# Third SAGE pass with the turn and copy of an older unit ahead of the step, and a head that adds half of its sums by an identity product

## The chip, the cores and the metric

The kernel runs on one core of one Trainium2 chip. The metric is the device time of one execution in microseconds; each kernel is run several times, and the median stands for it. One execution is also taken by the hardware profiler, and all the times inside a kernel come from that one trace: they are microseconds from the start of its span, or nanoseconds where that is said. TensorE is called PE, VectorE DVE, ScalarE ACT, GpSimd POOL and SyncE SP in the profile.

## What is computed

For 16 graphs of 1024 nodes with 128 features, two layers are applied, each as `x = layernorm(x + layer(x))`. The first is a gated graph network (a GRU over four steps). The second is three SAGE passes with batch norm between them, and a linear head on the three results side by side. Cut to the part that the change touches:

```python
def _sage(x, adj, Wr, Wx, b, mf):
    deg = jnp.clip(jnp.sum(adj, axis=-1, keepdims=True), 1.0, None)
    agg = jnp.einsum('bij,bjd->bid', adj, x) / deg
    out = agg @ Wr + x @ Wx + b
    nrm = jnp.maximum(jnp.linalg.norm(out, axis=-1, keepdims=True), NORM_EPS)
    return out / nrm * mf[..., None]

h3 = _bn(jax.nn.relu(_sage(h2, adj_d, Wr3, Wx3, b3, mf)), g3, be3)
xc = jnp.concatenate([h1, h2, h3], axis=-1) * mf[..., None]
return (xc @ Wl + bl) * mf[..., None]
...
x = _layernorm(x + _L1_gnn_ref(x, adj, nodemask, ...), axis=-1)
```

Batch norm takes its mean and variance over all the nodes of all the graphs, so the head can't begin before the third pass has ended.

## The kernel before

The order of the work on every engine is written out by hand: each engine executes its instructions in the order in which the code records them, and waits where one needs the result of another engine or a buffer that is still in use. The last three stages of the kernel are the third pass, a short set-up and the head.

**The third pass** (`third`, L1806) works on 32 units: 16 graphs times two halves `f` of 512 nodes. The products with the adjacency were made in the pass before and lie in DRAM; `load_layer` (L1693) fetches them for a graph, a graph ahead, on SP's queue. Step `i` of the loop does this, in this order:

- `out_next` (L1728) for unit i on TensorE: four products for the neighbours (`q_oa`, L1734), four of the degree row (`q_ob`, L1737) and four of the node itself against two weights at once (`q_ob`, L1740). A product of float32 stands in the trace as two records.
- `rows` (L1384 to L1391) for unit i-2 on VectorE: three small operations on the norms and one of 128x512 that makes the normalised rows `s_r`.
- `chain` (L1743) for unit i: ScalarE divides `q_oa` by the degree (`scale_rows`, L1370, four times), VectorE adds `q_ob` (L1373), ScalarE squares and sums (`squares`, L1380, four times, each with a record that reads the accumulator) and takes a root (L1381). Then VectorE adds the other half of `q_ob` to the running sums of the head (`s_acc`, L1833).
- for unit i-3: TensorE turns `s_r` (`turned`, L1402, four transposes), ScalarE copies the result out of PSUM into `r3` (L1837) and VectorE takes its batch-norm statistics (L1838).

The PSUM pool of the pass has two buffers each of `q_oa` (one bank), `q_ob` (two banks) and `s_tr` (one bank)[...].

**The set-up** (`batch_norm`, L1305 to L1310, and `head_weights`, L1347) aggregates the statistics, scales the head's third weight (`s_wr`, L1313) and makes `r48`, 48 rows for the constant part (L1320 to L1327), with small products between (`s_v`, L1355 and L1358).

**The head** (`last`, L1841) goes over the 16 graphs. For graph b, `head(b)` makes in each half four products of a mask with a row picked for the graph (`u_rb` by VectorE, L1853; products L1864) and four of `r3` with the weight (L1867), all into one bank `u_p`. VectorE adds `s_acc` to it (L1869), which gives `u_y`, and takes the layer norm's statistics, four of them (L1872) and four aggregates (L1874). ScalarE takes a root for the graph (L1876). `norm(b)`, recorded after `head(b + 1)`, makes scale and shift on VectorE (L1881, L1882), applies them on ScalarE in eight instructions of 128x128 (L1885) and sends 512 KB to the output on SP's queue (L1887). After it comes a flag (`flagged`, L1916).

Of the kernel before, what the change touches and what calls it, by code (L numbers as in the profile page):

```python
# [8 lines left out]
F32 = mybir.dt.float32  # L9
# [5 lines left out]
AF = mybir.ActivationFunctionType  # L15
ALU = mybir.AluOpType
AX = mybir.AxisListType
ET = mybir.EngineType
PSUM = bass.MemoryType.PSUM
DRAM = bass.MemoryType.DRAM  # L20

P = 128
B = 16
# [18 lines left out]
def rows_of(ap):  # L42

    return ap.rearrange("(k p) c -> p k c", p=P)
# [1149 lines left out]
class Sage:  # L1194
# [479 lines left out]
    def second(self):  # L1674

        nc, tc = self.nc, self.tc
        with ExitStack() as c:
            pool = lambda name, **k: c.enter_context(tc.tile_pool(name=name, **k))
            self.wk = pool("q_wk", bufs=2)
            self.big = pool("q_at", bufs=2)  # L1680
            self.ps1 = pool("q_ps1", bufs=1, space=PSUM)
            self.ps2 = pool("q_ps2", bufs=2, space=PSUM)
            c.enter_context(tc.manual_schedule(engines={ET.PE, ET.DVE, ET.Activation, ET.Pool, ET.SP}))
            last, self.g = self.g[B - 1], {}
            self.load_second(0)
            self.load_bytes(0, 0)
            for f in range(2):
                nc.sync.dma_start(self.ag[B - 1, f], last["ag2"][f])
            for b in range(B + 1):
                for t in range(8):  # L1690
                    self.slot_second(b, t)
# [114 lines left out]
    def third(self):  # L1806

        nc, tc = self.nc, self.tc
        with ExitStack() as c:
            pool = lambda name, **k: c.enter_context(tc.tile_pool(name=name, **k))  # L1810
            self.wk = pool("t_wk", bufs=3)
            self.ps2 = pool("t_ps2", bufs=2, space=PSUM)
            c.enter_context(tc.manual_schedule(engines={ET.PE, ET.DVE, ET.Activation, ET.Pool, ET.SP}))
            last, self.g = self.g[B - 1], {}
            self.load_layer(0)
            nc.sync.dma_start(self.rt[B - 1, 1], last["rt", 1])
            for f in range(2):
                nc.sync.dma_start(self.ag[B - 1, f], last["ag", f])
            units = [(b, f) for b in range(B) for f in range(2)]
            for i in range(len(units) + 3):  # L1820
                if i < len(units):
                    b, f = units[i]
                    if f == 0 and b + 1 < B:
                        self.load_layer(b + 1)
                    self.out_next(b, f, self.ps2)
                if 2 <= i < len(units) + 2:
                    b1, f1 = units[i - 2]
                    g = self.g[b1]
                    g["r", f1] = self.rows(b1, f1, g.pop(("o", f1)), g.pop(("ss", f1)))
                if i < len(units):  # L1830
                    pp = self.chain(b, f, True)
                    acc = self.acc[:, b, 4 * f:4 * f + 4, :]
                    nc.vector.tensor_add(acc, pp, acc)  # L1833
                if i >= 3:
                    b2, f2 = units[i - 3]
                    pt = self.turned(self.g[b2]["r", f2], self.ps2)
                    nc.scalar.copy(self.r3[:, b2, f2, :], pt)  # L1837
                    nc.vector.bn_stats(self.stats[2][:, 2 * b2 + f2, :], self.r3[:, b2, f2, :])  # L1838


    def last(self, r48):  # L1841
        nc, tc, cst = self.nc, self.tc, self.cst
        with ExitStack() as c:
            pool = lambda name, **k: c.enter_context(tc.tile_pool(name=name, **k))
            wk = pool("u_wk", bufs=6)
            ps = pool("u_ps", bufs=4, space=PSUM)
            c.enter_context(tc.manual_schedule(engines={ET.PE, ET.DVE, ET.Activation, ET.Pool, ET.SP}))
            st = {}

            def row(b):  # L1850
                if b < B:
                    st["row", b] = wk.tile([3 * B, C], BF, name="u_rb", bufs=3)
                    nc.vector.tensor_scalar(st["row", b], r48, self.graph[:, b:b + 1], None, op0=ALU.mult)  # L1853

            def head(b):
                rb = st.pop(("row", b))
                row(b + 1)
                y = wk.tile([P, NB, C], F32, name="u_y")
                mv = self.small.tile([P, NB, 2], F32, name="p_mv")
                for f in range(2):  # L1860
                    pp = ps.tile([P, 4, C], F32, name="u_p")
                    for i in range(4):
                        k = 4 * f + i
                        nc.tensor.matmul(pp[:, i, :], self.mask48[:, k * P:(k + 1) * P], rb,  # L1864
                                         start=(i == 0), stop=False)
                    for i in range(4):
                        nc.tensor.matmul(pp[:, i, :], self.r3[:, b, f, i * P:(i + 1) * P], self.wr2,  # L1867
                                         start=False, stop=(i == 3))
                    nc.vector.tensor_add(y[:, 4 * f:4 * f + 4, :], pp, self.acc[:, b, 4 * f:4 * f + 4, :])  # L1869
                    s6 = self.small.tile([P, 4, 6], F32, name="p_st")  # L1870
                    for i in range(4):
                        nc.vector.bn_stats(s6[:, i, :], y[:, 4 * f + i, :])  # L1872
                    for i in range(4):
                        nc.vector.bn_aggr(mv[:, 4 * f + i, :], s6[:, i, :])  # L1874
                rs = self.small.tile([P, 2, NB], F32, name="u_rs")
                nc.scalar.activation(rs[:, 0, :], mv[:, :, 1], AF.Sqrt, bias=self.eps)  # L1876
                st[b] = y, mv, rs

            def norm(b):
                y, mv, rs = st.pop(b)  # L1880
                nc.vector.reciprocal(rs[:, 0, :], rs[:, 0, :])  # L1881
                nc.vector.scalar_tensor_tensor(rs[:, 1, :], mv[:, :, 0], -1.0, rs[:, 0, :],  # L1882
                                               op0=ALU.mult, op1=ALU.mult)
                for k in range(NB):
                    nc.scalar.activation(y[:, k, :], y[:, k, :], AF.Identity, bias=rs[:, 1, k:k + 1],  # L1885
                                         scale=rs[:, 0, k:k + 1])
                nc.sync.dma_start(rows_of(self.out[b]), y)  # L1887

            row(0)
            for b in range(B + 1):  # L1890
                if b < B:
                    head(b)
                if b:
                    norm(b - 1)
# [107 lines left out]
```

## Time and profile before

| | us |
|---|---|
| three executions | 2422.9, 2425.41, 2429.3 |
| the profiled execution | 2424.86 |
| its span in the trace | 2423.1 |
| third pass, from its first product to its last statistics | 2184.2 to 2337.4 |
| set-up | 2337.4 to 2343.3 |
| head, up to the end of its last ScalarE instruction | 2343.3 to 2416.9 |
| end of the span | 2423.1 |

Over the whole span PE is busy 93%, DVE 80%, ACT 57% and POOL 42%. These shares are means over stages with different limits, and say little of the two stages here. By windows, busy us of the engines:

| window | us | PE | DVE | ACT | POOL | clock granted to PE |
|---|---|---|---|---|---|---|
| 2205 to 2325, steady third pass | 120.00 | 106.56 | 79.41 | 78.63 | 0.00 | 1.00 |
| 2337.44 to 2343.30, set-up | 5.86 | 1.63 | 3.93 | 0.29 | 0.00 | 0.50 |
| 2363.12 to 2371.10, two graphs of the head | 7.98 | 5.79 | 7.77 | 6.83 | 0.00 | 1.00 |

A line of the timeline has the start, the duration, the engine, the line of the code, the operation, output and inputs by the program's names, the shapes and, in brackets, for how long the engine had been idle and who released it. Neighbours on an engine overlap a little, so the time that an instruction takes on a full engine is the distance of its start from the next start, not its duration.

### The profile page before, as it was taken

The page shows a single profiled execution, that of the slowest core. Times are in us where ns is not written, and L with a number is a line of the kernel's source. Part 1 is how long each engine was busy: PE and PEld are TensorE (multiplying, and loading weights), DVE is VectorE, ACT ScalarE, POOL GpSimd, SP SyncE. Part 2 cuts the span into 40 slices and gives each one's busy share as a digit, 9 for nine tenths or more (in the row PEclk, how much of TensorE's full clock was granted, in tenths as well). Part 3 has the DMA queues.
Part 4 walks back from the last instruction along what each step waited for, and adds up shares of the span by engine and source line. Part 5 has one row for each costly group of instructions (what it writes and reads, how often), then busy time and mean ns, then how long its engine had stood idle before and what let it go on. Part 6 is the DMA issues. An engine that isn't in the chain of part 4 may idle for free.

```text
span 2423.1 us, 35665 instructions
## 1 busy us (share of the span) xinstructions
PE 2260.7 (93%) x11897; PEld 1558.2 (64%) x11913; DVE 1927.9 (80%) x4153; ACT 1384.0 (57%) x3228; POOL 1014.2 (42%) x937
## 2 busy tenths in 40 slices
PE   6999999999999999999998699999999899989875
PEld 4666555666556656566555477777777677777654
DVE  4998998989989989899899677777777466665677
ACT  3566556565565555565655466665666354545647
POOL 3335244353352442533523566666666244440000
PEclk9999999999999999999999799999999899999988
DMA  7337253364271643632722777887775466645404
GB/s 257 110 99 256 68 207 125 124 226 125 90 245 57 224 132 118 217 119 95 260 69 84 280 274 269 295 287 282 269 271 216 173 234 223 232 149 172 123 9 132
DMA packets 214389, 436.17 MB, mean 180 GB/s; under 512 B 59570, under 2 KB 80724, under 8 KB 214196
## 3 DMA queue, kind: packets, MB, share of 16 engines
q1 hardware_dynamic: 186756, 345.96, 41.5%
q0 software_dynamic: 23040, 83.90, 10.2%
q10 hardware_dynamic: 4400, 3.95, 0.5%
q8 instruction: 96, 1.57, 0.3%
q14 instruction: 97, 0.79, 0.1%
HBM read 324.49 MB, written 109.25 MB: 179 GB/s over the span
## 4 chain that ended last, share of the span: by engine, by line
PE 49%; DVE 22%; ACT 12%; DMA 8%; issue 6%; POOL 3%; SPq 0%; DVEq 0%; ACTq 0%; POOLq 0%
PE h_g L1089 12%; PE p_ag L1543 9%; PE h_g L1077 9%; DVE f_rank L735 4%; DMA e_sum<-h_x 3%; ACT s_junk L1380 2%; PE q_ag L1776 2%; PE p_u L1470 2%; PE p_u L1471 2%; PE p_u L1464 2%; ACT f_u L909 2%; DMA h_a<-in_adj_dram 2%; DVE f_x L893 2%; PE q_ob L1740 2%; PE s_tr L1402 1%
## 5 line engine op out<-in xcount | busy, mean ns | idle before, releaser
L1089 PE MATMUL h_g<-h_h,h_wh 128*128 128x512 f32 x768 | 397.7, 599 | 3.6 <-DVE h_r L1102 3.5
L1089 PE MATMUL h_g<-h_ms,h_wi 128*128 128x512 f32 x768 | 392.3, 592 | 0.0
L1479 POOL CAST p_b<-p_at 128x512 uint8<-128x512 f32 x256 | 256.3, 1021 | 129.5 <-ACT p_at L1472 129.4
L735 DVE TENSOR_TENSOR_SCAN f_rank<-f_a,f_first,f_pd 128x1024 f16<-128x1024 f32 x128 | 299.3, 2344 | 3.3
L1077 PE MATMUL h_g<-h_a,h_hi 128*128 128x512 f32 x1024 | 284.0, 417 | 7.5 <-DMA h_a<-in_adj_dram 7.4
L1118 POOL TENSOR_TENSOR h_h<-h_zh,h_r 128x512 f32<-128x512 f32 x128 | 184.7, 1443 | 198.1 <-DVE h_r L1117 170.7
L1472 ACT ACTIVATE p_at<-p_u,s_less 128x512 fp32r<-128x512 f32 x256 | 175.9, 688 | 157.9 <-PE p_u L1471 154.3
L1089 PEld LDWEIGHTS h_g<-h_ms,h_wi 128*128 128x128 f32 x768 | 145.5, 190 | 184.3 <-issue 164.2
L1077 PE MATMUL h_g<-h_a,h_lo 128*128 128x512 f32 x1024 | 262.0, 393 | 0.0
L1077 PEld LDWEIGHTS h_g<-h_a,h_hi 128*128 128x128 f32 x1024 | 188.3, 188 | 71.5 <-issue 20.3
L863 DVE SCALAR_TENSOR_TENSOR f_nr<-f_u,f_q,f_a 128x1024 bf16<-128x1024 f16 x128 | 183.8, 1453 | 57.1 <-ACT f_u L912 50.4
L1112 POOL TENSOR_TENSOR h_zh<-h_z,h_h 128x512 f32<-128x512 f32 x64 | 81.6, 1275 | 323.7 <-ACT h_z L1108 323.7
L1077 PEld LDWEIGHTS h_g<-h_a,h_lo 128*128 128x128 f32 x1024 | 189.9, 188 | 38.3
L1488 DVE SCALAR_TENSOR_TENSOR p_a<-p_a 128x1024 bf16<-128x1024 f32 x128 | 209.9, 1679 | 3.1 <-DMA p_a<-in_adj_dram 3.1
L1380 ACT ACTIVATE s_junk<-s_o 128x128 bf16<-128x128 f32 x384 | 113.7, 298 | 128.7 <-DVE s_o L1373 128.7
L1089 PEld LDWEIGHTS h_g<-h_h,h_wh 128*128 128x128 f32 x768 | 129.1, 190 | 86.7 <-issue 68.3
L1105 ACT ACTIVATE h_r<-h_r,h_bi 128x512 f32<-128x512 f32 x128 | 92.4, 722 | 140.8 <-DVE h_r L1104 140.8
L1080 ACT COPY h_ms<-h_g 128x512 f32<-128x512 f32 x128 | 73.9, 577 | 173.0 <-PE h_g L1077 129.9
L909 ACT ACTIVATE f_u<-f_rank,f_q 128x128 f16<-128x128 f16 (+7 forms) x128 | 110.6, 867 | 75.1 <-DVE f_rank L849 75.1
L1470 PE MATMUL p_u<-ident_b,p_a 128*128 128x128 bf16 x1024 | 144.9, 222 | 4.0 <-DMA p_a<-in_adj_dram 3.0
L1471 PE MATMUL p_u<-ident_b,p_nr 128*128 128x128 bf16 x1024 | 144.9, 222 | 0.0
L1740 PE MATMUL q_ob<-s_wxp,q_xt 128*128 128x256 f32 x512 | 130.8, 399 | 0.0
(243 smaller groups left out, 4942.2 us busy)
## 6 DMA issues: line engine op xcount, KB each, us to landing
h_a<-in_adj_dram POOLq DMA_DIRECT2D x128, 512.0 KB, 7.4
p_a<-in_adj_dram SPq DMA_DIRECT2D x128, 512.0 KB
f_a<-in_adj_dram SPq DMA_DIRECT2D x124, 512.0 KB
e_nr<-f_nr SPq DMA_DIRECT2D x128, 256.0 KB
p_nr<-e_nr SPq DMA_DIRECT2D x32, 1024.0 KB
s_at<-p_b SPq DMA_DIRECT2D x32, 512.0 KB
s_ag<-s_ag SPq DMA_DIRECT2D x64, 256.0 KB
q_agi<-s_ag SPq DMA_DIRECT2D x32, 512.0 KB
```

What stands on the lines that cost most here:

```text
L735: nc.vector.tensor_tensor_scan(out, a, other[:, 0, 0:1].to_broadcast([P, N]), start, op0=ALU.add, op1=ALU.bypass)
L863: nc.vector.scalar_tensor_tensor(nr, self.us[g], self.q[:, 2, g:g + 1], self.a[g], op0=ALU.not_equal, op1=ALU.is_ge)
L1077: nc.tensor.matmul(pm[f], part[:, j, :], st.adj[j][:, half[f]], start=(j == 0 and n == 0), stop=(j == NB - 1 and n == 1))
L1089: nc.tensor.matmul(pg, lhs, rhs, start=(i == 0), stop=(i == len(mm) - 1))
L1118: nc.gpsimd.tensor_tensor(h, zh, r, ALU.subtract)
L1470: nc.tensor.matmul(pu[:, i * P:(i + 1) * P], a[:, blk, 1], ib, start=False, stop=False)
L1471: nc.tensor.matmul(pu[:, i * P:(i + 1) * P], nr[:, k, blk], ib, start=False, stop=(i == 3))
L1472: nc.scalar.activation(g["at"][:, j, cols], pu, AF.Relu, bias=self.less2)
L1479: self.nc.gpsimd.tensor_copy(g["b", f][:, j, :], g["at"][:, j, f * HF:(f + 1) * HF].bitcast(F32))
L1488: self.nc.vector.scalar_tensor_tensor(low, a, 0.0, a, op0=ALU.is_gt, op1=ALU.not_equal, accum_out=self.bad[:, c:c + 1])
L1543: self.nc.tensor.matmul(pa, hi[:, j, :], at[:, j, f * HF:(f + 1) * HF], start=(start and n == 0), stop=(stop and n == len(js) - 1))
L1740: nc.tensor.matmul(pb[:, i], g["xt"][:, f, blk], self.wxp, start=False, stop=(i % 2 == 1))
```

## The change

In the third pass the turn and the copy of unit i-3 are recorded at the beginning of step i, ahead of `out_next`, and its statistics after `rows` and ahead of `chain`. In the head, the products of `r3` come ahead of those of the mask; in the second half of a graph (`f` = 1) the running sums are added by a product with the identity on TensorE, in PSUM, in place of VectorE's addition, and the statistics and the normalisation read PSUM; the mask rows are made on GpSimd, two graphs ahead in place of one; one of the eight normalisations of a graph goes to GpSimd, and three of the last graph's to VectorE; the PSUM pool has eight buffers in place of four.

```diff
@@ third
             for i in range(len(units) + 3):
+                if i >= 3:
+                    b2, f2 = units[i - 3]
+                    pt = self.turned(self.g[b2].pop(("r", f2)), self.ps2)
+                    nc.scalar.copy(self.r3[:, b2, f2, :], pt)
                 if i < len(units):
...
                     self.out_next(b, f, self.ps2)
...
                     g["r", f1] = self.rows(b1, f1, g.pop(("o", f1)), g.pop(("ss", f1)))
+                if i >= 3:
+                    nc.vector.bn_stats(self.stats[2][:, 2 * b2 + f2, :], self.r3[:, b2, f2, :])
                 if i < len(units):
                     pp = self.chain(b, f, True)
                     acc = self.acc[:, b, 4 * f:4 * f + 4, :]
                     nc.vector.tensor_add(acc, pp, acc)
-                if i >= 3:
-                    b2, f2 = units[i - 3]
-                    pt = self.turned(self.g[b2]["r", f2], self.ps2)
-                    nc.scalar.copy(self.r3[:, b2, f2, :], pt)
-                    nc.vector.bn_stats(self.stats[2][:, 2 * b2 + f2, :], self.r3[:, b2, f2, :])
@@ last
-            ps = pool("u_ps", bufs=4, space=PSUM)
+            ps = pool("u_ps", bufs=8, space=PSUM)
...
-                    nc.vector.tensor_scalar(st["row", b], r48, self.graph[:, b:b + 1], None, op0=ALU.mult)
+                    nc.gpsimd.tensor_scalar(st["row", b], r48, self.graph[:, b:b + 1], None, op0=ALU.mult)
...
-                row(b + 1)
+                row(b + 2)
...
                     pp = ps.tile([P, 4, C], F32, name="u_p")
+                    for i in range(4):
+                        nc.tensor.matmul(pp[:, i, :], self.r3[:, b, f, i * P:(i + 1) * P], self.wr2,
+                                         start=(i == 0), stop=False)
+                    if f:
+                        nc.tensor.matmul(pp.rearrange("p a b -> p (a b)"), cst["ident"],
+                                         acc.rearrange("p a b -> p (a b)"), start=False, stop=False)
                     for i in range(4):
                         k = 4 * f + i
                         nc.tensor.matmul(pp[:, i, :], self.mask48[:, k * P:(k + 1) * P], rb,
-                                         start=(i == 0), stop=False)
-                    for i in range(4):
-                        nc.tensor.matmul(pp[:, i, :], self.r3[:, b, f, i * P:(i + 1) * P], self.wr2,
-                                         start=False, stop=(i == 3))
-                    nc.vector.tensor_add(y[:, 4 * f:4 * f + 4, :], pp, self.acc[:, b, 4 * f:4 * f + 4, :])
+                                         start=False, stop=(i == 3))
+                    if not f:
+                        nc.vector.tensor_add(y[:, :4, :], pp, acc)
...
+                    src = pp if f else y
                     for i in range(4):
-                        nc.vector.bn_stats(s6[:, i, :], y[:, 4 * f + i, :])
+                        nc.vector.bn_stats(s6[:, i, :], src[:, i, :])
...
                 for k in range(NB):
-                    nc.scalar.activation(y[:, k, :], y[:, k, :], AF.Identity, bias=rs[:, 1, k:k + 1],
-                                         scale=rs[:, 0, k:k + 1])
+                    src = pp[:, k - 4, :] if k > 3 else y[:, k, :]
+                    scale, shift = rs[:, 0, k:k + 1], rs[:, 1, k:k + 1]
+                    if k == 0:
+                        nc.gpsimd.tensor_scalar(y[:, k, :], src, scale, shift, op0=ALU.mult, op1=ALU.add)
+                    elif b == B - 1 and k % 2 == 0:
+                        nc.vector.tensor_scalar(y[:, k, :], src, scale, shift, op0=ALU.mult, op1=ALU.add)
+                    else:
+                        nc.scalar.activation(y[:, k, :], src, AF.Identity, bias=shift, scale=scale)
...
             row(0)
+            row(1)
```

More of the change, by code (lines that the diff above doesn't have):

```diff
@@ L1860, in head @@
                 for f in range(2):
+                    acc = self.acc[:, b, 4 * f:4 * f + 4, :]
                     pp = ps.tile([P, 4, C], F32, name="u_p")
+                    for i in range(4):
[4 more added lines that the diff above has]
+                                         acc.rearrange("p a b -> p (a b)"), start=False, stop=False)
                     for i in range(4):
@@ L1864, in head @@
                         nc.tensor.matmul(pp[:, i, :], self.mask48[:, k * P:(k + 1) * P], rb,
-                                         start=(i == 0), stop=False)
-                    for i in range(4):
-                        nc.tensor.matmul(pp[:, i, :], self.r3[:, b, f, i * P:(i + 1) * P], self.wr2,
-                                         start=False, stop=(i == 3))
-                    nc.vector.tensor_add(y[:, 4 * f:4 * f + 4, :], pp, self.acc[:, b, 4 * f:4 * f + 4, :])
-                    s6 = self.small.tile([P, 4, 6], F32, name="p_st")
-                    for i in range(4):
-                        nc.vector.bn_stats(s6[:, i, :], y[:, 4 * f + i, :])
+                                         start=False, stop=(i == 3))
+                    if not f:
+                        nc.vector.tensor_add(y[:, :4, :], pp, acc)
+                    s6 = self.small.tile([P, 4, 6], F32, name="p_st")
+                    src = pp if f else y
+                    for i in range(4):
+                        nc.vector.bn_stats(s6[:, i, :], src[:, i, :])
                     for i in range(4):
@@ L1876, in head @@
                 nc.scalar.activation(rs[:, 0, :], mv[:, :, 1], AF.Sqrt, bias=self.eps)
-                st[b] = y, mv, rs
+                st[b] = y, pp, mv, rs
             def norm(b):
-                y, mv, rs = st.pop(b)
+                y, pp, mv, rs = st.pop(b)
                 nc.vector.reciprocal(rs[:, 0, :], rs[:, 0, :])
```

## Prediction, before the result was known

> **What bounds the kernel now.** I read the page for the totals, then the table of windows to find the two stages that the change touches: the third pass runs from 2184.0 to 2337.4 us of the span, the head's set-up to 2343.3, the head to 2416.9. They are 233 of 2423 us; nothing else is edited. Then the list of waits for the middle of the third pass (columns: waiter, releaser, total us, times, longest):
>
> ```profile
> ACT s_junk L1380 <- DVE s_o L1373: 43.5, 29, 1.5
> DVE s_st L1838 <- ACT s_r L1837: 40.8, 28, 1.5
> PE s_tr L1402 <- DVE s_r L1391: 17.0, 24, 3.9
> ```
>
> ScalarE and VectorE wait for each other once in every step and TensorE waits too, so no engine is full: it is a ring. The timeline of one step shows it (start, duration, instruction, idle before):
>
> ```profile
> 2260.64 0.31 ACT L1380 ACTIVATE s_junk<-s_o 128x128 bf16<-128x128 f32 x1 [1.52 <-DVE s_o L1373]
> ...
> 2262.07 0.57 ACT L1837 COPY s_r<-s_tr 128x512 f32<-128x512 f32 x1
> 2262.53 1.15 ACT L1370 ACTIVATE s_o<-q_oa,s_rdeg 128x128 f32<-128x128 f32 x4
> ...
> 2262.67 0.69 DVE L1838 BATCH_NORM_STATS2 s_st<-s_r 128x6 f32<-128x512 f32 x1 [1.46 <-ACT s_r L1837]
> ...
> 2264.49 0.68 DVE L1373 TENSOR_TENSOR s_o<-q_ob,s_o 128x512 f32<-128x512 f32 x1
> ```
>
> From L1373 the ring goes to the squares (L1380), the root and the copy (L1837), then the statistics (L1838), the four operations of `rows` (to L1391) and the next L1373. It takes 4.56 us: squares start at 2260.64 and next at 2265.20. Early in the pass TensorE, not yet held back, shows what it needs:
>
> ```profile
> 2200.39 0.60 PE L1402 MATMUL s_tr<-ident,s_r 128*128 128x128 f32 x4
> ...
> 2204.18 0.60 PE L1402 MATMUL s_tr<-ident,s_r 128*128 128x128 f32 x4
> ```
>
> 3.79 us from one turn to the next, without a gap. In the head the timeline of VectorE is back to back and everybody else waits for it; TensorE waits on the mask row:
>
> ```profile
> 2370.77 0.24 DVE L1853 TENSOR_SCALAR u_rb<-s_r,s_graph 48x128 bf16<-48x128 bf16 x1
> 2370.93 0.67 DVE L1869 TENSOR_TENSOR u_y<-u_p,s_acc 128x512 f32<-128x512 f32 x1
> ...
> 2374.75 0.24 DVE L1853 TENSOR_SCALAR u_rb<-s_r,s_graph 48x128 bf16<-48x128 bf16 x1
> ```
>
> ```profile
> 2371.06 0.39 PE L1864 MATMUL u_p<-u_rb,s_mask 48*128 48x128 bf16 x4 [1.09 <-DVE u_rb L1853]
> 2371.39 1.16 PE L1867 MATMUL u_p<-s_wr,s_r 128*128 128x128 f32 x8
> 2372.48 0.39 PE L1864 MATMUL u_p<-u_rb,s_mask 48*128 48x128 bf16 x4
> ```
>
> So a graph costs 3.98 us, set by VectorE; a half costs TensorE 1.42 us.
>
> [...] the head's matmuls start at 2343.63 on a clock of 0.50 and reach 1.00 at 2350.4. [...] the add from PSUM (L1373) takes 0.68 us, L1391 on the same size from SBUF 0.69. [...]
>
> **Part 1, the third pass.** The turn and copy of unit i-3 go ahead of the step's other work; its statistics go between `rows` and L1373. No instruction is added, and the SP loads keep their order. Three rings remain. VectorE alone: L1373 0.60, L1833 0.61, `rows` 1.21, statistics 0.61 (start to start) = 3.03 us. ScalarE with L1373: squares and root 1.42, copy 0.46, L1370 1.15, L1373 and the two hand-overs 0.77 = 3.80 us; the sum is checked by the first steps, where the same ring without a copy takes 3.32 to 3.35. TensorE: 3.79. The statistics leave the ring: they start when the copy ends, 0.6 us before L1370 does, and need 0.61. The new waits: the turn waits for `s_r`, made a step earlier; the copy waits for the turn, and behind it on ScalarE stand L1370 and the squares. The turn is issued 0.2 us before L1373 of the step before and takes 0.6, the copy's place comes 2.1 us after that L1373, so 1.7 us are spare. I take 3.80.
>
> L1373 runs at 2200.66 in step 3 and at 2328.30 in step 31. After: step 3 at about 2201.1 (the copy now precedes it), and 28 x 3.80 = 106.4 more, 2307.5: 20.8 us saved. Drain: from that L1373 to the final aggregate (L1305, 2337.44) 9.1 us now, since each of three units queues turn, copy, statistics and `rows` in one line; overlapped I count squares 2.0, copy 0.6, statistics 0.6, `rows` 1.3, last turn, copy and statistics 2.2 = 6.7. Saved 2.4. **Together 23.2.**
>
> **Part 2, the head's rate.** VectorE loses the mask (0.16) and one add (0.71) a graph: 3.98 - 0.87 = 3.11. Statistics on PSUM are not in the trace[...]. ScalarE loses one of eight normalisations of 0.40 (start to start): 0.23 + 7 x 0.40 = 3.0[...]. GpSimd gets one 48x128 mask and one 128x128 normalisation: nearest rows 0.31 (128x128 select, L662) and 1.94 (48x3 select, L1267), so 0.6 to 3.9 a graph; I take 0.8. TensorE gains the identity product, f32 128x512. The GRU stage's product of that shape (L1089, one float32 weight tile of 128x128 in each) takes two records and 0.85 us from issue to issue:
>
> ```profile
> 1000.09 1.02 PE L1089 MATMUL h_g<-h_h,h_wh 128*128 128x512 f32 x2
> 1000.94 1.02 PE L1089 MATMUL h_g<-h_ms,h_wi 128*128 128x512 f32 x2
> ```
>
> TensorE then needs 2 x 1.42 + 0.85 = 3.69 us: it becomes the bound, and the head's gain is 0.29 a graph, not 0.87. Its weights load beside the product before (L1089 shows no gap). Masks are made two graphs ahead; a mask waits behind a normalisation that waits for the root two instructions before, about 2.5 us after a graph's products, while it is needed 3.7 later still. Eight banks hold four graphs, and ScalarE gives one back within two.
>
> **Part 3, the head's ends.** Start: products of `r3` now precede the mask and need only `s_wr` and a free bank, at 2341.9 (end of L1321) instead of 2343.63, both in the old trace's time. The array is cold for 5 to 7 us then, at a rate near 0.55 (L1867 x8 takes 2.07 instead of 1.16). Products end at 2341.9 + 16 x 3.69 + 0.45 x 6 + 0.3 for the first mask = 2403.9. Then statistics and aggregates 1.2, root and scale 0.6, the seven normalisations of graph 14 at 0.39, four of graph 15 (three go to VectorE, one to GpSimd, beside them): 2403.9 + 1.8 + 2.7 + 1.6 = 2410.0. Now they are one line of sixteen:
>
> ```profile
> 2410.62 6.26 ACT L1885 ACTIVATE u_y<-u_y,u_rs 128x128 f32<-128x128 f32 x16
> ```
>
> It ends at 2416.9: **6.9 us saved**, and the last transfer (6.2 us to the end) is unchanged. The output transfers keep their place on SP; 512 KB per 3.7 us is 142 GB/s, the page has slices of 290.
>
> **Sum:** 2423.1 - 23.2 - 6.9 = 2393.0 for the profiled span. That execution took 2424.9; the three runs went from 2422.9 to 2429.3 with a median 2.3 above the span: **2395 us**. About 0.3% (7 us, from 2418 on) is what a measurement can tell from no change.
>
> **Rivals.** (B) The head gives nothing per graph: GpSimd at the slow end (3.9 us) or the identity product a third dearer keeps 3.98. For: no row shows the GpSimd operations; against: 128x128 there took 0.31. Part 1, plus 2.0 for the shorter last line (4.3 for 6.3) and 0.4 of the earlier start: 2425.4 - 23.2 - 2.4 = 2400. (C) The third pass finds a new ring: copy waiting for a turn that TensorE, now full, gives late. For: two rings within 0.01 us of each other and the copy at the head of ScalarE's queue; against: 1.7 us to spare. At half of the gain (4.18 a step) 2406, with no step gained 2416. (D) Slower: the array never warms in the head. [...]the clock stays at 0.50, a graph costs 2 x 2.54 + 1.70 = 6.8 and the products end 47 us later: 2442. It [...]loses to the old kernel from 5.6 us a graph. Against: with gaps of 1.09 in each 3.98 us the old head kept 1.00.
>
> **How the numbers follow.** Forecast 0.70, B 0.13, C 0.12 (a sixth of it within 0.3%), D 0.03, other 0.02. The forecast's own spread: clock 1.5 either way, VectorE and GpSimd unknowns up to +4, third-pass hand-overs 0.1 a step = +3, runs -2 to +4: 2389 to 2401. To hold 8 in 10 it takes in B and the near part of C: 2389 to 2405. Faster 0.95, same 0.02, slower 0.03.
>
> **What would show it.** Right: squares 3.8 us apart in the third pass; ScalarE's wait for L1373 down from 1.5 to about 0.7; TensorE without gaps there; in the head TensorE back to back at 3.7 us a graph and VectorE waiting for `u_p`; a last line of eleven normalisations or so. Wrong: steps over 4 us with a copy waiting for its turn, a head whose matmuls wait for GpSimd, or a clock below 1.00 past its first 7 us.

## The result, and the profile after

The changed kernel takes **2398.3 us** (median of 4 runs, 2397.2 to 2402.0) against 2426.4 us for the kernel before (4 runs); the ratio is 0.9887, with a 95% interval from 0.987 to 0.9905. The forecast was 2395, range 2389 to 2405, so the time lies in the range, 3.3 us above the forecast. The profiled span went from 2423.1 to 2396.1 us; 2393.0 was forecast.

Both spans can be cut at the same two instructions: the final aggregate of the third pass (L1305) and the end of ScalarE's last normalisation. All starts and ends are from the timelines.

| stage | before | after | difference | forecast |
|---|---|---|---|---|
| third pass, first L1373 to L1305 | 146.75 | 123.41 | -23.3 | -23.2 |
| head, L1305 to the end of the last normalisation | 79.44 | 72.02 | -7.4 | -6.9 |
| from there to the end of the span | 6.25 | 9.59 | **+3.3** | 0 |

What comes before the third pass is not edited, but it moves that pass's start by up to 7 us between the profiled runs shown below (2189.3 to 2196.2). So the stages are compared here rather than the whole spans. In the profiled run of the kernel after it starts 0.4 us later than in that of the kernel before; with that, the three lines make up the 3.1 us by which the span misses its forecast.

**Third pass.** The list of waits of the kernel after, for the middle of the pass (waiter, releaser, total us, times, longest):

```profile
ACT s_junk L1380 <- DVE s_o L1373: 22.0, 29, 0.8
DVE s_o L1373 <- ACT s_o L1370: 10.2, 29, 0.4
DVE s_st L1836 <- ACT s_r L1825: 7.1, 29, 0.2
```

The squares still wait for VectorE in each step, but 0.76 us instead of 1.52, and TensorE is gone from the list apart from its own issue time. One step in the timeline of the kernel after (start, duration, instruction, idle before):

```profile
2258.09 0.60 PE L1402 MATMUL s_tr<-ident,s_r 128*128 128x128 f32 x4
...
2259.09 0.31 ACT L1380 ACTIVATE s_junk<-s_o 128x128 bf16<-128x128 f32 x1 [0.76 <-DVE s_o L1373]
...
2260.51 0.57 ACT L1825 COPY s_r<-s_tr 128x512 f32<-128x512 f32 x1
2260.97 1.15 ACT L1370 ACTIVATE s_o<-q_oa,s_rdeg 128x128 f32<-128x128 f32 x4
2261.11 0.69 DVE L1836 BATCH_NORM_STATS2 s_st<-s_r 128x6 f32<-128x512 f32 x1 [0.25 <-ACT s_r L1825]
...
2261.88 0.60 PE L1402 MATMUL s_tr<-ident,s_r 128*128 128x128 f32 x4
...
2262.16 0.69 DVE L1373 TENSOR_TENSOR s_o<-q_ob,s_o 128x512 f32<-128x512 f32 x1 [0.35 <-ACT s_o L1370]
...
2262.88 0.31 ACT L1380 ACTIVATE s_junk<-s_o 128x128 bf16<-128x128 f32 x1 [0.76 <-DVE s_o L1373]
```

From squares to squares it is 3.79 us, and from turn to turn 3.79. The copy does not wait for its turn (the turn ended at 2258.69, the copy starts at 2260.51), and the statistics run beside L1370.

**Head.** The same view for one graph in the middle of it:

```profile
2346.99 1.16 PE L1866 MATMUL u_p<-s_wr,s_r 128*128 128x128 f32 x8
2347.09 0.89 DVE L1881 BATCH_NORM_STATS2 p_st<-u_p 128x6 f32<-128x128 f32 x4 [0.40 <-PE u_p L1874]
...
2348.07 0.40 PE L1874 MATMUL u_p<-u_rb,s_mask 48*128 48x128 bf16 x4
...
2348.40 1.16 PE L1866 MATMUL u_p<-s_wr,s_r 128*128 128x128 f32 x8
...
2349.08 0.60 POOL L1855 TENSOR_SCALAR u_rb<-s_r,s_graph 48x128 bf16<-48x128 bf16 x1
2349.23 0.87 DVE L1881 BATCH_NORM_STATS2 p_st<-u_y 128x6 f32<-128x128 f32 x4
...
2349.39 1.02 PE L1870 MATMUL u_p<-s_acc,ident 128*128 128x512 f32 x2
...
2350.35 0.39 PE L1874 MATMUL u_p<-u_rb,s_mask 48*128 48x128 bf16 x4
...
2350.68 1.16 PE L1866 MATMUL u_p<-s_wr,s_r 128*128 128x128 f32 x8
```

TensorE follows itself without an idle bracket and repeats after 3.69 us (2346.99, 2350.68). VectorE, which had been back to back, now waits 0.40 us for each second half.

**The end.** The last lines of the same timeline:

```profile
2384.34 0.88 ACT L1901 ACTIVATE u_y<-u_y,u_rs 128x128 f32<-128x128 f32 x2
...
2385.59 0.41 DVE L1899 TENSOR_SCALAR u_y<-u_p,u_rs 128x128 f32<-128x128 f32 x1 [2.51 <-ACT u_y L1901]
2386.04 0.46 ACT L1901 ACTIVATE u_y<-u_p,u_rs 128x128 f32<-128x128 f32 x1 [0.48 <-DVE u_y L1899]
...
2386.55 0.19 PE L1942 MATMUL l_sum<-l_col,l_max 128*1 128x1 f32 x2 [6.28 <-ACT u_y L1901]
2386.78 0.15 DVE L1944 TENSOR_SCALAR l_flag<-l_sum 1x1 int32<-1x1 f32 x1 [0.77 <-PE l_sum L1942]
```

The normalisations end at 2386.5, but 9.6 us follow. The next work is the product for the flag that decides whether the general path has to run, and it waited 6.28 us for ScalarE. Then every engine loads the flag and jumps over the general path (L1985 in the kernel after, L1969 before). The answer for that line in the kernel after (queue, operation, count: duration in ns, first and last start; EVENT_SEMAPHORE is what an engine does first behind the jump):

```profile
L1985 SPq EVENT_SEMAPHORE  x8: 17/17/17, 2392.3 to 2392.8; - x8
...
L1985 POOLq COMPARE_BRANCH  x1: 45/45/45, 2387.5 to 2387.5; - x1
L1985 SPq COMPARE_BRANCH  x1: 50/50/50, 2387.5 to 2387.5; - x1
...
L1985 POOLq EVENT_SEMAPHORE  x1: 17/17/17, 2392.3 to 2392.3; - x1
```

and in the kernel before:

```profile
L1969 SPq EVENT_SEMAPHORE  x8: 17/17/17, 2420.9 to 2421.4; - x8
L1969 POOLq COMPARE_BRANCH  x1: 45/45/45, 2412.4 to 2412.4; - x1
...
L1969 POOLq EVENT_SEMAPHORE  x1: 17/17/17, 2415.9 to 2415.9; - x1
...
L1969 SPq COMPARE_BRANCH  x1: 50/50/50, 2417.9 to 2417.9; - x1
```

The branch itself is recorded with 0.05 to 0.08 us (on TensorE with 3.57 before and 4.03 after), but the next instruction of the same engine comes 3.0 to 4.8 us later. Before, the flag was ready at 2411.8, in the middle of ScalarE's last line: the other engines jumped beside it, and only SP, which had to issue the last output transfer first, jumped behind it, in 3.0 us (2417.9 to 2420.9). After, all five jump together behind the last normalisation, in 4.8 us (2387.5 to 2392.3). And behind its jump GpSimd has a DRAIN, a record of the sequencer that the trace gives 2.85 us; before, it was over at 2418.8, 2.1 us ahead of the end of SP's jump, after, it stands at the very end. So the two ends add up like this, from the records of the trace:

| | before | after |
|---|---|---|
| last normalisation to the branch (SP's; after, GpSimd's) | 1.01 | 1.03 |
| jump | 3.00 (SP alone) | 4.78 (GpSimd's, with all five) |
| from there to the end of the span | 2.24 (SP's semaphores) | 3.78 (GpSimd's drain of 2.85 in it) |
| sum | 6.25 | 9.59 |

What moves in the gap of the kernel after is in the table of DMA queues for 2387.6 to 2392.2 (queue, kind: packets, MB, share of 16 engines):

```profile
q1 hardware_dynamic: 982, 0.49, 35.6%
q14 instruction: 4, 0.03, 1.8%
q8 instruction: 1, 0.02, 1.6%
```

Beside the last of the output, whose last packet starts at 2389.1, these are five packets of instructions, as many as there are engines. They start at 2389.0 to 2389.1, 1.4 to 1.5 us behind the branches, and the longest is over at 2390.2, while the engines go on at 2391.6 to 2392.4. In the kernel before, four such packets start at 2413.4 to 2414.0, behind the four early branches, and one at 2419.3, behind SP's.

### The profile page after: what moved, and what is told of

Same layout as the page of the kernel before. It is cut to its first block, busy times and chain, and to the rows that moved or that the text cites. A ratio compares the mean times of both kernels' runs of the same rounds, so it can differ in the third digit from the quotient of the medians.

```text
span 2396.1 us, 35746 instructions
## 1 busy us (share of the span) xinstructions
PE 2269.5 (95%) x11945; PEld 1563.5 (65%) x11945; DVE 1920.4 (80%) x4124; ACT 1374.1 (57%) x3209; POOL 1031.8 (43%) x969
## 4 chain that ended last, share of the span: by engine, by line
PE 52%; DVE 19%; ACT 14%; DMA 8%; issue 5%; POOL 3%; SPq 0%; DVEq 0%; ACTq 0%; POOLq 0%
PE h_g L1089 12%; PE p_ag L1543 10%; PE h_g L1077 9%; DVE f_rank L735 4%; DMA e_sum<-h_x 3%; ACT s_junk L1380 3%; PE q_ag L1776 2%; PE p_u L1464 2%; PE p_u L1471 2%; PE p_u L1470 2%; ACT f_u L909 2%; DMA h_a<-in_adj_dram 2%; DVE f_x L893 2%; DVE s_o L1373 1%; DVE f_a L727 1%
```

## The experiments

All stages below are cut as in the table above: third pass | head | end, in us of the profiled run. A time without an interval is that of a single run.

**1 and 2: each part of the change alone.** The kernel before with the whole edit of `third` and the old head, and with the old third pass and the whole edit of `last`.

```diff
@@ e1, third of the change only
+                if i >= 3:
+                    b2, f2 = units[i - 3]
+                    pt = self.turned(self.g[b2].pop(("r", f2)), self.ps2)
+                    nc.scalar.copy(self.r3[:, b2, f2, :], pt)
...
+                    nc.vector.bn_stats(self.stats[2][:, 2 * b2 + f2, :], self.r3[:, b2, f2, :])
@@ e2, last of the change only
-            ps = pool("u_ps", bufs=4, space=PSUM)
+            ps = pool("u_ps", bufs=8, space=PSUM)
...
```

> The third pass of the changed kernel with the head of the kernel before. Theory (the parts add up, the ring of the third pass is the source of most of the gain): steps of 3.79 us, 23.0 us off up to the batch norm's aggregate, the head unchanged at 3.98 us a graph and the end unchanged at 6.2 us after the last normalisation: a span near 2400 us, 23 us less than before. Rival (the faster third pass was partly bought by the head's change, by its PSUM pool or its masks on GpSimd): less than 20 us.

> The head of the changed kernel behind the third pass of the kernel before. Theory (the head gains 7.4 us up to its last normalisation and gives 3.4 us of it back after it, because the flag's product now waits for that normalisation and the branches come after it): 4 us less than before, a span near 2419, with 9.6 us from the last normalisation to the end. Rival (the late end belongs to the earlier or faster third pass, or is chance): 6.2 us there, and a span near 2416.

The third pass alone: 2405.4 us, ratio 0.991 (0.9893 to 0.9926), stages 124.6 | 79.5 | 6.2. The head alone: 2422.7 us, ratio 0.9986 (0.9979 to 0.9993), stages 147.7 | 73.0 | 9.6. Multiplied, the two ratios give 0.9896, within the interval of the whole change, and each stage is within 1.2 us of its place in the whole change; so the parts add up, and the loss at the end belongs to the head: of the 6.5 us that its edit saves up to the last normalisation, the end takes back 3.3. Alone it makes the kernel 3.7 us faster (2426.4 to 2422.7).

**3 and 4: which of the two moves in the third pass opens the ring.** In e3 the turn and the copy stay where they were and only the statistics are made one step later; in e4 turn and copy lead as in the change, and the statistics come at the end of the step. Both have the old head.

```diff
@@ e3, against the kernel before
+                if i >= 4:
+                    b3, f3 = units[i - 4]
+                    nc.vector.bn_stats(self.stats[2][:, 2 * b3 + f3, :], self.r3[:, b3, f3, :])
                 if i < len(units):
...
                     nc.scalar.copy(self.r3[:, b2, f2, :], pt)
-                    nc.vector.bn_stats(self.stats[2][:, 2 * b2 + f2, :], self.r3[:, b2, f2, :])
@@ e4, against the third of the change
-                if i >= 3:
-                    nc.vector.bn_stats(self.stats[2][:, 2 * b2 + f2, :], self.r3[:, b2, f2, :])
                 if i < len(units):
...
+                if i >= 3:
+                    nc.vector.bn_stats(self.stats[2][:, 2 * b2 + f2, :], self.r3[:, b2, f2, :])
```

> The kernel before, with one VectorE instruction of a step moved: the batch-norm statistics of the third pass are taken a step later, after rows and ahead of chain; turn and copy stay at the end of the step. Theory (the ring went through the statistics because they stood ahead of rows on VectorE): steps of 3.8 us, about 21 us less than before, nearly the whole gain of the third pass. Rival (the turn and copy leading the step is what gives the gain): steps stay at 4.56 us and the span at 2423.

> The kernel before, with turn and copy at the beginning of the step as in the changed kernel, and the statistics left at its end. Theory (VectorE no longer stands behind the copy when it comes to rows, since the copy is made before the squares): steps of 3.8 us here too, about 21 us less than before. Rival (only the statistics' place counts): 4.56 us a step, or above 4 us.

Both have steps of 3.79 to 3.80 us: e3 123.5 | 80.5 | 6.3 (2407.1 us), e4 124.2 | 80.1 | 6.2 (2401.5 us). The waits of e3 in the middle of the pass:

```profile
ACT s_junk L1380 <- DVE s_o L1373: 22.0, 29, 0.8
DVE s_o L1373 <- ACT s_o L1370: 11.1, 29, 0.8
```

and of e4:

```profile
ACT s_junk L1380 <- DVE s_o L1373: 22.0, 29, 0.8
DVE s_o L1373 <- ACT s_o L1370: 20.8, 29, 1.3
```

The wait of the squares is 22.0 us in both, as with the whole change. The old ring went through copy *and* statistics in line; taking either out of the line is enough, and what is left is ScalarE's own ring and TensorE's 3.79. The change does both, and the second one brings nothing more to the step. (Head and end are the old code in these two: 80.5 and 80.1 against 79.4 to 79.7 elsewhere. The rate is the same 3.98 to 3.99; what differs is the start. The clock granted to TensorE went from 0.50 back to 1.00 at 16.1 and 15.3 us after the start of L1305 here, and at 12.9 to 13.5 us in the other three runs with the old head.)

**5: the flag early.** The product and the comparison for the flag are made ahead of the third pass (its input is complete by then); loading it and branching stay at the end.

```diff
         with tc.tile_pool(name="s_psw", bufs=1, space=PSUM) as ps:
             self.weights(2, ps)
+        flag_early(tc, flag, self.bad)
...
-    with tc.If(flagged(tc, one, bad) > 0):
+    with tc.If(flagged(tc, flag) > 0):
```

> The kernel after, with the flag's product and comparison made ahead of the third pass; only the load of the flag and the branch stay at the end. If the 3.4 us lost behind the last normalisation are TensorE's branch, which came late because the flag's product stood behind ScalarE's last normalisation, TensorE branches right behind its last product (about 2380, done by 2385, ahead of the last normalisation at 2386), and the time from the last normalisation to the end of the span goes from 9.6 back to about 6.2: span about 2392.7, median about 2395. Rival: the end is late because the output's transfers are crowded or because VectorE and ScalarE wait for each other in the last graph; then the 9.6 us stay and the time is that of the kernel after, 2398.3.

2395.4 us (2394.6 to 2400.6), ratio 0.9869 (0.9853 to 0.9886), stages 124.3 | 72.0 | 6.3. The end is back at its old length, 3.3 us less, and the other stages are unmoved; the profiled span is 2398.8 only because the third pass started at 2196.2 there, 5.2 later than in the kernel after (with the same edit it started at 2191.0 in experiment 6 and at 2189.9 in 11, so the edit is not the reason). The interval overlaps with that of the kernel after, so the gain rests on the stages, where it is clear. The flag's line is L1990 in this run:

```profile
L1990 SPq EVENT_SEMAPHORE  x8: 17/17/17, 2396.6 to 2397.1; - x8
L1990 PEldq COMPARE_BRANCH  x1: 3890/3890/3890, 2384.2 to 2384.2; - x1
...
L1990 POOLq COMPARE_BRANCH  x1: 45/45/45, 2389.2 to 2389.2; - x1
L1990 POOLq EVENT_SEMAPHORE  x1: 17/17/17, 2391.8 to 2391.8; - x1
...
L1990 SPq COMPARE_BRANCH  x1: 50/50/50, 2393.5 to 2393.5; - x1
```

Each engine now jumps when its own work is done: TensorE at 2384.2, GpSimd at 2389.2 (it goes on at 2391.8; with 2.85 us of drain, as in the kernel after, that is over at about 2394.8, an estimate), SP last and in 3.1 us. My expectation named TensorE's branch, whose record is 4.0 us long in the kernel after, as what is paid. That was too narrow: TensorE's was over at 2388.2 here, and ScalarE, VectorE and SP still needed 3.1 to 3.3 us each. The price is the jump on every engine; what was lost is that five of them, and GpSimd's drain, moved behind the last normalisation.

**6: the same in the kernel before**, as a control, with the same edit.

```diff
+        flag_early(tc, flag, self.bad)
```

> The kernel before, with the flag's product and comparison ahead of the third pass. There the branch is hidden behind ScalarE's last line of sixteen normalisations already: the time from the last normalisation to the end stays 6.2 us and the stages keep 146.7 and 79.5 us. If the early flag were worth its 3.3 us whatever the head, the last part would fall to about 3 us.

2425.5 us, stages 146.8 | 79.7 | 6.2. Nothing changes: where the jumps of the other engines are hidden already, making TensorE's earlier (now at 2405.0) is worth nothing; SP's own, at 3.0 us, stays.

**7: what holds the flag back.** Two waits stand ahead of it in the kernel after: TensorE's for ScalarE, and that of VectorE, whose flag instruction is queued behind its own normalisation that waits 2.51 us. In e9 the last graph is split so that the two engines don't alternate.

```diff
-                    elif b == B - 1 and k % 2 == 0:
+                    elif b == B - 1 and k < 4:
```

> The kernel after, with one edit: of the last graph VectorE normalises blocks 1, 2 and 3 (from SBUF) and ScalarE 4 to 7 (from PSUM), in place of every second one each. If the flag is late because its product waits for the PSUM bank that ScalarE's last normalisation reads, TensorE's branch stays behind that normalisation: the alternation of the two engines on one bank goes (0.5 us of wait and 0.2 less to do, last normalisation 0.7 us earlier), and the time from it to the end stays at 9.6 us. Rival: the flag is late because VectorE's flag instruction stands behind its own normalisation that waits 2.5 us for ScalarE; then that time goes back to about 6.3 us.

Stages 124.4 | 71.6 | 9.5 (2397.5 us). The end of its timeline:

```profile
2383.42 2.88 ACT L1901 ACTIVATE u_y<-u_p,u_rs 128x128 f32<-128x128 f32 x8
...
2386.35 0.19 PE L1942 MATMUL l_sum<-l_col,l_max 128*1 128x1 f32 x2 [5.62 <-ACT u_y L1901]
2386.57 0.14 DVE L1944 TENSOR_SCALAR l_flag<-l_sum 1x1 int32<-1x1 f32 x1 [2.84 <-PE l_sum L1942]
```

VectorE now has nothing of its own to wait for and stands idle for 2.84 us until TensorE delivers; TensorE still waits for ScalarE's last normalisation, and the end stays at 9.5. So the rival falls. The product reads nothing of ScalarE's (`l_col`, `l_max`), so by the code what is left is the place of its result in PSUM: the head's pool has grown to eight buffers there, and ScalarE still reads one of them. In e6 below, with the same eight buffers but no PSUM read by ScalarE, the same product runs at 2384.15, 3.5 us ahead of the last normalisation's end. So it is ScalarE's reading of PSUM that holds it back; whether it would also do so with four buffers was not tried.

**8 to 10: what bounds the head.** Without the identity product, with VectorE adding both halves and all normalisations from SBUF (e6); without it and without anything in its place (e7); with the masks back on VectorE (e8).

```diff
@@ e6, against the kernel after
-                    if f:
-                        nc.tensor.matmul(pp.rearrange("p a b -> p (a b)"), cst["ident"],
-                                         acc.rearrange("p a b -> p (a b)"), start=False, stop=False)
...
-                    if not f:
-                        nc.vector.tensor_add(y[:, :4, :], pp, acc)
+                    nc.vector.tensor_add(y[:, 4 * f:4 * f + 4, :], pp, acc)
...
-                    src = pp[:, k - 4, :] if k > 3 else y[:, k, :]
+                    src = y[:, k, :]
@@ e7, against the kernel after
-                    if f:
-                        nc.tensor.matmul(pp.rearrange("p a b -> p (a b)"), cst["ident"],
-                                         acc.rearrange("p a b -> p (a b)"), start=False, stop=False)
@@ e8, against the kernel after
-                    nc.gpsimd.tensor_scalar(st["row", b], r48, self.graph[:, b:b + 1], None, op0=ALU.mult)
+                    nc.vector.tensor_scalar(st["row", b], r48, self.graph[:, b:b + 1], None, op0=ALU.mult)
```

> The kernel after, with both halves of the sums added on VectorE and all normalisations from SBUF; no identity product, masks still on GpSimd. If the identity product is what moves the head's bound from VectorE to TensorE, TensorE falls to 2 x 1.42 = 2.84 us a graph and VectorE, 3.29 us busy in the kernel after plus 0.7 for the second sum, becomes the bound at about 3.9 to 4.0 us: the head some 4 us longer than after's 72.0 us (third pass's end to last normalisation, fixed parts included), near before's 79.4 less what the masks took from VectorE. Rival: the masks on GpSimd brought the gain and the identity product none: then the head stays at 72 us or is shorter.

> The kernel after without the identity product: the running sums of blocks 4 to 7 are left out of the output. If TensorE bounds the head at 3.69 us a graph, the rate falls to VectorE's own work of about 3.3 us: about 0.4 x 14 = 5 to 6 us off the 72.0 us of the head. Rival: VectorE or ScalarE already bound it (a full ring around the two), and nothing changes: 72 us.

> The kernel after with the 48x128 masks made on VectorE as before. VectorE's 3.29 us a graph plus 0.16 stay under TensorE's 3.69, so with TensorE as the bound the head stays at 72 us within 0.5. Rival: VectorE is in effect the bound (its waits of 0.4 us are handovers that can't be filled), and the head grows by 0.16 x 16, 2 to 3 us.

| | us a graph | head | end | time |
|---|---|---|---|---|
| before | 3.98 | 79.4 | 6.2 | 2426.4 |
| e6: masks on GpSimd, no identity product | 3.84 | 73.4 | 7.1 | 2400.2 |
| after: both | 3.69 | 72.0 | 9.6 | 2398.3 |
| e8: identity product, masks on VectorE | 3.69 | 72.3 | 9.3 | 2400.5 |
| e7: product left out | 3.13 | 62.7 | 9.7 | 2388.5 |

The rate is from one reciprocal (`u_rs`) of VectorE to that of the next graph. In e6 VectorE is back to back again (2348.64 and 2352.48 are the first additions of two graphs in a row) and TensorE is the one that waits:

```profile
2348.64 0.69 DVE L1872 TENSOR_TENSOR u_y<-u_p,s_acc 128x512 f32<-128x512 f32 x1
...
2349.89 0.38 PE L1870 MATMUL u_p<-u_rb,s_mask 48*128 48x128 bf16 x4 [0.95 <-POOL u_rb L1855]
...
2352.48 0.69 DVE L1872 TENSOR_TENSOR u_y<-u_p,s_acc 128x512 f32<-128x512 f32 x1
```

3.84 is before's 3.98 less the mask. My expectation of 3.9 to 4.0 was wrong, because I had added busy times, in which VectorE's instructions overlap; from start to start they come to less. e7 shows the same: its statistics have no wait for PSUM any more,

```profile
2347.24 0.69 DVE L1873 TENSOR_TENSOR u_y<-u_p,s_acc 128x512 f32<-128x512 f32 x1
...
2349.02 0.87 DVE L1877 BATCH_NORM_STATS2 p_st<-u_p 128x6 f32<-128x128 f32 x4
...
2350.37 0.69 DVE L1873 TENSOR_TENSOR u_y<-u_p,s_acc 128x512 f32<-128x512 f32 x1
```

and VectorE alone needs 3.13 us, not the 3.3 that I expected, so 9.3 us go off the head and not 5 to 6. That settles the bound: TensorE with the identity product holds the head at 3.69, and the masks, on whichever of the two engines, don't touch it (e8). The product exchanges VectorE's 3.84 for TensorE's 3.69. In the head e6 is 1.4 us slower than the kernel after, and at its end 2.5 faster, because its flag doesn't wait: the two kernels' times can't be told apart (e6 ratio 0.9893, 0.9876 to 0.9909). Of the 7.1 us at e6's end 6.2 are the usual ones; of the rest, 0.7 is SP's jump, 3.7 us there, soon after the four others had jumped together at 2385.4 to 2385.5.

**11: a version made from these.** The flag early, the last graph split by blocks, and the identity product for two of the four blocks only, so that TensorE and VectorE come closer to each other.

```diff
-                        nc.tensor.matmul(pp.rearrange("p a b -> p (a b)"), cst["ident"],
-                                         acc.rearrange("p a b -> p (a b)"), start=False, stop=False)
+                        nc.tensor.matmul(pp[:, 2:, :].rearrange("p a b -> p (a b)"), cst["ident"],
+                                         acc[:, 2:, :].rearrange("p a b -> p (a b)"), start=False, stop=False)
...
-                    if not f:
-                        nc.vector.tensor_add(y[:, :4, :], pp, acc)
+                    n = 2 if f else 4
+                    nc.vector.tensor_add(y[:, 4 * f:4 * f + n, :], pp[:, :n, :], acc[:, :n, :])
...
-                    elif b == B - 1 and k % 2 == 0:
+                    elif b == B - 1 and k < 4:
```

> Flag early, the last graph split by blocks, and the identity product over two of four blocks (6 and 7) only; VectorE adds the other two. With TensorE at 2.84 + half of 0.85 = 3.27 us a graph and VectorE at 3.13 (its rate where the product was left out) plus 0.37 for a 128x256 addition = 3.50, the head goes at 3.50 in place of 3.69: 15 x 0.19 = 2.8 us and 0.7 at its end, head 68.4 us, end 6.3 us: about 6.8 us less than the kernel after, median about 2391.5. Rival: two dependences in the second half (a shorter addition, then statistics from two places) cost VectorE what is saved, and the head stays at 3.69: median 2394.5.

**2391.7 us** (2391.3 to 2395.0), ratio 0.9866 (0.9849 to 0.9882), stages 124.0 | 69.8 | 6.3. Against the kernel after that is 2.2 us less in the head and 3.3 at the end. The rate is 3.58 and not 3.50, and the timeline shows where the 0.08 is:

```profile
2377.61 0.39 DVE L1877 TENSOR_TENSOR u_y<-u_p,s_acc 128x256 f32<-128x256 f32 x1
...
2378.04 0.49 DVE L1880 BATCH_NORM_STATS2 p_st<-u_y 128x6 f32<-128x128 f32 x2
2378.44 0.48 DVE L1880 BATCH_NORM_STATS2 p_st<-u_p 128x6 f32<-128x128 f32 x2
```

The half-size addition holds VectorE for 0.43 us from start to start, not for half of the 0.72 of a whole one (I had taken 0.37), and the statistics in two groups hold it for 0.80 (to the next instruction at 2378.84), not 0.78. The two intervals overlap a little, so as with experiment 5 it is the stages that show the gain; 0.4 us of the head's is what the split alone gave in experiment 7. That the median meets the 2391.5 of the expectation is partly luck: the head is 1.4 us longer than expected, and in the profiled run the third pass started 1.2 us earlier than in the kernel after.

## Why the prediction was right, and where not

- **What bounds the third pass**: right. The ring of 4.56 us was what held it; experiments 3 and 4 break it at two places and find the same 3.80 below.
- **Part 1, the step of 3.80 and the drain**: right to 0.2 us in sum (23.2 against 23.3). That ScalarE's ring (3.80) and TensorE (3.79) meet there was in the sum, and the trace shows both: turns at 3.79 with no idle time, squares at 3.79 with 0.76 of wait. Which of the two would hold the pass alone was not tried.
- **Part 2, TensorE becomes the bound at 3.69**: right, 3.69 in each graph, and experiments 8 to 10 show it is TensorE. VectorE's 3.11 was 3.13 (e7), although half of its statistics come from PSUM. What those cost could not be read from the trace of before; four of them take 0.89 us in the kernel after and 0.87 in e7, against 0.87 from SBUF. ScalarE's normalisations are a little shorter from PSUM: eight take 2.88 us in e9 with 0.46 for a single one, seven from SBUF 2.80 in e6 with 0.48 for a single one, which makes 0.35 and 0.39 from start to start, 0.04 us less each. GpSimd's two operations, taken at 0.8, took 0.60 and 0.45, 1.05 together; no engine stood idle behind them in the steady head of the kernel after. (The 1.94 us behind the upper end of their range was the mean of two selects, of 0.18 and 3.70 us.) Beside GpSimd's work VectorE's addition and statistics take 0.69 and 0.87 us; in the kernel before, with GpSimd idle, it was 0.67 and 0.87.
- **Part 3, the start and the normalisations' end**: right, 7.4 us for 6.9. The products of `r3` start 4.6 us behind the start of L1305 (2319.05, 2314.47), forecast was 4.5 (2341.9, 2337.44), but the clock stayed at 0.50 for only 4.5 us from there (to 2323.5), not for 5 to 7. The last product ends 65.8 us after the start of L1305 where 66.5 were forecast, which covers the half microsecond gained beyond the forecast. The same head behind the old third pass (e2) had the clock at 0.50 for 6.5 us, and took 73.0.
- **"the last transfer (6.2 us to the end) is unchanged"**: this is the step that failed. I took the 6.2 us for the transfer's and their change for nothing, without asking what else stood between the last normalisation and the end, and what the rest of that work was hidden behind. It is the jump over the general path: SP's 3.0 us of it were in the 6.2, the other engines' jumps were hidden behind a line of sixteen normalisations, and GpSimd's drain behind that line and SP's last work. The change shortens that line, and by reading PSUM in it, it puts the flag's product behind the line's end. The cost is 3.3 us: 1.8 for five jumps together instead of SP's alone, 1.5 for the drain. Experiment 5 takes it back (6.3 us), 6 shows that the same edit is worth nothing in the kernel before, and 7 that the wait is TensorE's and not VectorE's. What an engine does in the gap behind its jump is not shown. In these two kernels one packet of instructions follows each jump before the engine goes on, but in the kernel after all five are over at 2390.2 and the first engine goes on at 2391.6, 1.4 us later, so these packets alone don't fill the gap. Not tried were a kernel without the branch, and what makes the five jumps of the kernel after longer than SP's alone before (4.8 us against 3.0): that their packets move together (from 2389.0 to 2389.1 on), or that the last of the output moves until then.
- **The rivals**: B would have given 2400 and C 2406 to 2416. The measured 2398.3 lies closer to B's 2400 than to 2395, and still B did not happen: the head gained its 0.29 a graph, and 3.3 us were lost in another place. The time alone would have pointed to the wrong cause. D did not happen either; the clock was at 1.00 from the second graph on (2324.8).

## What to carry to other kernels

When work on the last stretch is shortened, list everything that the old end hid, instructions that are not counted as busy among them: the load of a flag, branches, a drain, a product that waits for a place in PSUM. A price of nothing needs the name of what hides it, looked up in the changed order. And where work is handed from one engine to another, stop where the two meet: here the identity product for two blocks of a graph gave 3.58 us a graph, for four 3.69.

## What was not expected of the hardware

- A conditional branch over a long stretch of code is recorded with 0.05 to 0.08 us on four engines, but each goes on only 2.6 to 4.1 us later in runs where not all five jump together (before, e5, e6, e10), and 4.6 to 4.8 us later where all five jump at once (after, e9). On TensorE the record itself is long (3.6 to 4.3 us in these runs). Why the jumps are longer there is open; jumping together is not the only way to a long one, since in e5b GpSimd, alone at 2182.5, went on only 5.2 us later.
- Behind the jump GpSimd has a drain, of 2.84 us in the kernel before and 2.85 in the kernel after.
- On GpSimd the smaller operation is the dearer one: the 48x128 bf16 mask takes 0.60 us, the 128x128 float32 normalisation 0.45. On VectorE the mask took 0.24.
